# Position tile laid out with the table index outermost: column terms of a relative-position bias read back in 1 KB runs

## The chip, the cores and the metric

The kernel runs on one core of a Trainium2 chip. The metric is the device time of one execution in microseconds (us); less is better. A core has TensorE (PE) for matmuls, with its weight loads shown apart (PEld), VectorE (DVE), ScalarE (ACT), GpSimd (POOL), and SyncE (SP), which here only issues transfers. Transfers are carried by 16 DMA engines that all issuing queues share.

## What is computed

Two layers of attention with relative positions, each over 4 images of 32 x 32 positions and 768 channels, 12 heads of 64. For every layer (the first has no qkv bias and no scale on q inside the position terms; otherwise the same):

```
x   = x + attention(groupnorm(x))              # 32 groups of 24 channels
qkv = xn @ Wqkv (+ bias)                       # q, k, v: (B*12, 1024, 64)
rel_h[q=(h,w), kh] = q . Rh[h - kh + 31]       # table of 63 rows of 64
rel_w[q=(h,w), kw] = q . Rw[w - kw + 31]
scores = scale * q @ k.T + rel_h[..., :, None] + rel_w[..., None, :]
out = softmax(scores) @ v @ Wproj + bproj
```

The row term rel_h depends on the query's row h and the key's row; the column term rel_w on the query's column w and the key's column. In the second layer the tables have 27 rows, and the host's table is widened to 63 columns by repeating its edge.

## The kernel before

Everything is float32. The outer order is image by image, layer by layer (8 images in all), in an image the 6 pairs of heads (48 pairs, g), and in a pair 8 blocks of 128 queries (n = 0 to 7). A pair and a block is a unit of work: 384 of them, some 8.6 us each. The order of all instructions on all engines is written out by hand in the loop over the units; nothing is rescheduled. Matrix products for projections are split in Strassen's manner (products, values, combine, sums), which is why GpSimd subtracts weights (L133, L144) and adds inputs (L311).

In the iteration of unit u, in this order: SP issues what earlier iterations put off (the lists early and later); GpSimd computes the biases of unit u+2 (L521); TensorE computes the scores of u+1 (L535); VectorE adds score and bias and takes the row extreme (L547), ScalarE takes exponentials (L551); TensorE does a share of projections (L342, L370, L427) of the next pair; VectorE transposes the probabilities of u in blocks of 32 (L571) into tb, SP writes tb to a DRAM tile td (L573); VectorE takes reciprocals (L559) and ScalarE, in two of eight units GpSimd for one head, scales the probabilities of u+1 (L565, L563). One or two iterations later SP reads td back, turned, into pt (L582), and at n = 6 and at n = 2 of the next pair TensorE multiplies pt with v (L600, av). tb has two buffers, td five, sc six.

A matmul chain is split into two halves between which a small operation of VectorE or ScalarE on the weights (L331, L329) orders the halves.

Position terms, made twice a pair, half i for the blocks 4i to 4i+3 (96 halves in all):

- positions (L462): TensorE multiplies q of the pair with the table, 8 matmuls (L473), into a PSUM tile of (query, head h, block j, 128 table columns: 64 for rows, 64 for columns). ScalarE copies the 64 columns that belong to column terms into t (L478), and a window of the row columns into raw (L481). The PSUM tile comes from the pool ps_m, which has two buffers and also serves projections and av.
- place_positions (L486): ScalarE issues the write of t to a DRAM tile tdr (L488), 128 rows of 512 B per block, and copies raw into the row terms of the tile rel, four copies of 32 partitions (L496), for each of the four rows of a block of queries a window shifted by one.
- diagonals (L499), put off to a later iteration: for query column w the column terms are 32 table columns that begin at 31 - w. Reading tdr with a step between partitions of one row less one element turns that into a plain copy. Each read has 32 partitions, 4 blocks and 32 elements: runs of 128 B, 8 transfers (2 heads x 4 rows of queries) of 16 KB each, issued on SP (in the very first half four of them on ScalarE).
- biases (L514): for each head, row term plus column term, both repeated, to a full 128 x 1024 tile. Keys are kept in an order in which the column index splits into l (8) and a (4), so the column operand is read with a step of 4 elements (16 B).

SP's transfers and those of ScalarE use eight landing counters in turn: the program makes a transfer wait until the one that used its counter before, eight transfers earlier, has landed.

Of the kernel before, what the change touches and what calls it, by code (L numbers as in the profile page):

```python
# [31 lines left out]
FP = mybir.dt.float32  # L32
# [4 lines left out]
P = 128  # L37
B, HW, C = 4, 32, 768
S = HW * HW
# [6 lines left out]
HALF = 512  # L46
# [5 lines left out]
WIDE = HW + 4  # L52
# [4 lines left out]
def attention_blocks(ctx: ExitStack, tc: tile.TileContext, a: dict, out: bass.AP):  # L57
    nc = tc.nc
# [10 lines left out]
    tmppool = ctx.enter_context(tc.tile_pool(name="tmp", bufs=1))  # L69
    tbpool = ctx.enter_context(tc.tile_pool(name="tb", bufs=2))  # L70
    ptpool = ctx.enter_context(tc.tile_pool(name="pt", bufs=2))
    relpool = ctx.enter_context(tc.tile_pool(name="rel", bufs=3))
# [5 lines left out]
    dram2 = ctx.enter_context(tc.tile_pool(name="scratch2", bufs=2, space=bass.MemoryType.DRAM))  # L78
# [78 lines left out]
    for sign, base in ((1, 0), (-1, GS // NC - 1)):  # L157
        nc.gpsimd.affine_select(
            out=same_group, in_=same_group, pattern=[[-sign * (GS // NC), NG], [0, GS // NC]],
# [15 lines left out]
    for l in range(LAYERS):  # L175
        tab = const.tile([P, 2, 2 * HW], FP, tag=f"tab{l}", name=f"tab{l}")
        nc.gpsimd.memset(tab, 0.0)
        for i, ax in enumerate("hw"):
            src = a[f"rel{ax}{l}"]
            n = src.shape[1]  # L180
# [10 lines left out]
    for l in range(LAYERS):  # L191
        t = const.tile([P, NC], FP, tag=f"bo{l}", name=f"bo{l}")
# [121 lines left out]
    qk_of, v_of, rel_of, t_of = {}, {}, {}, {}  # L314
# [33 lines left out]
    def products(g, kind):  # L348
# [44 lines left out]
        if kind == 0:  # L393
            nc.scalar.copy(kept, ts[0])
            add(turned(qs[0]), ts[1], kept, 0)
            early_positions.append(lambda: positions(g, 0))
        elif kind == 1:
            add(ks[0], ts[0], kept)
            add(ks[1], ts[1], ks[0])
        elif kind == 2:  # L400
            add(turned(qs[1]), ts[1], ks[1], 0)
            add(ks[0], ts[0], ks[0])
            add(ks[1], ts[0], ks[1], 1)
        else:
            add(ks[0], ts[0], ks[0], 1)
            add(ks[0], ts[1], ks[0])
            if g + 1 < NPAIR:
                later.append(lambda: load_w(g + 1, "c"))
# [53 lines left out]
    def positions(g, i):  # L462

        l = images[g // NP][0]
        q = qk_of[g, 0]
        if i == 0:
            t_of[g] = dram2.tile([S, P], FP, tag="tdr", name=f"tdr_{g}")
        ps = ps_m.tile([P, 2, 4, P], FP, tag="m", name=f"tp_{g}_{i}")
        for j in range(4):
            for h in range(2):  # L470
                rows = slice(h * D, (h + 1) * D)
                at = 4 * i + j
                nc.tensor.matmul(  # L473
                    ps[:, h, j, :], lhsT=q[rows, at * P : (at + 1) * P], rhs=tabs[l][rows, :],
                    start=True, stop=True,
                )
        t = tmppool.tile([P, 4, 2, 2 * HW], FP, tag="tmp", name=f"t_{g}_{i}")
        nc.scalar.copy(t, ps[:, :, :, 2 * HW :].rearrange("p h j r -> p j h r"))  # L478
        raw = tmppool.tile([P, 2, 4, WIDE], FP, tag="raw", name=f"raw_{g}_{i}")
        first = ps[:, :, 0, 2 * HW - WIDE - 4 * 4 * i : 2 * HW - 4 * 4 * i]  # L480
        nc.scalar.copy(  # L481
            raw, bass.AP(first.tensor, first.offset, [first.ap[0], first.ap[1], [P - 4, 4], [1, WIDE]])
        )
        return lambda: place_positions(g, i, t, raw)

    def place_positions(g, i, t, raw):  # L486

        nc.scalar.dma_start(  # L488
            out=t_of[g][i * HALF : (i + 1) * HALF, :].rearrange("(j p) r -> p j r", p=P),
            in_=t.rearrange("p j h r -> p j (h r)"),  # L490
        )
        rel = relpool.tile([P, 2, 2, 4, HW], FP, tag="rel", name=f"rel_{g}_{i}")
        rel_of[g, i] = rel
        for y in range(4):
            rows = slice(y * HW, (y + 1) * HW)
            nc.scalar.copy(rel[rows, :, 0, :, :], raw[rows, :, :, WIDE - 1 - HW - y : WIDE - 1 - y])  # L496
        later.append(lambda: diagonals(g, i))

    def diagonals(g, i):  # L499
        td = t_of[g]  # L500
        for h in range(2):
            for y in range(4):
                src = bass.AP(
                    td.tensor, td.offset + (4 * i * P + HW * y) * P + h * 2 * HW + HW - 1,
                    [[P - 1, HW], [P * P, 4], [1, HW]],
                )
                (nc.scalar if h and not g + i else nc.sync).dma_start(
                    out=rel_of[g, i][y * HW : (y + 1) * HW, h, 1, :, :], in_=src
                )


    sc_of, st_of, tb_of, pt_of, attn_of = {}, {}, {}, {}, {}

    def biases(g, n):  # L514
        rel, m = rel_of[g, n // 4], n % 4
        for h in range(2):
            sc = scpool.tile([P, HW, HW], FP, tag="sc", name=f"sc_{g}_{n}_{h}")
            sc_of[g, n, h] = sc

            shape = [P, 4, HW, 8]  # L520
            nc.gpsimd.tensor_tensor(  # L521
                sc.rearrange("p (a k) (u l) -> p a (k u) l", a=4, l=8),
                rel[:, h, 0, m, :].unsqueeze(1).unsqueeze(3).to_broadcast(shape),
                rel[:, h, 1, m, :].rearrange("p (l a) -> p a l", a=4).unsqueeze(2).to_broadcast(shape),
                ALU.add,
            )

# [247 lines left out]
    with tc.manual_schedule(engines=ENGINES):  # L775
# [31 lines left out]
        load_w(1, "a")  # L807
        now["G3"].part()
        positions(0, 1)()
        run(later)  # L810
        run(later)
        ahead = prepare(1)
        fetch(3)
        biases(0, 0)
        scores(0, 0)()
        ahead["G0"].part()
        ahead["G0"].between()
        divide(0, 0)
        biases(0, 1)
        held = []  # L820
        same = {
# [10 lines left out]
        for at, (g, n) in enumerate(units):  # L832
# [37 lines left out]
            if at + 2 < len(units):  # L870
                biases(*units[at + 2])
# [3 lines left out]
            if n == 7 and g + 1 < NPAIR:  # L875
                placing.append(positions(g + 1, 1))
# [118 lines left out]
```

## Time and profile before

| | |
|---|---|
| median of 3 runs | 3310.84 us (3309.95 to 3312.62) |
| the profiled execution | 3317.11 us, of which the span of instructions is 3314.9 us |
| mean granted clock of TensorE | 1.0 |
| busy share | PE 99%, DVE 77%, POOL 72%, ACT 60% |
| transfers | 1047.38 MB in 524,180 packets, 316 GB/s; SP's and ScalarE's queue together take 89% of 16 DMA engines |
| diagonal reads (rel<-tdr) | 764 on SP and 4 on ScalarE, 16 KB each, 4.2 us from issue to landing (median on SP) |
| write of t (tdr<-t) | 96 on ScalarE, 256 KB each, 6.4 us to landing |

A group line has the kernel's line, engine, operation, what is written and read with shapes, and the count; after the first bar the busy time in us and the mean of one in ns; after the second the engine's idle time just before such instructions and what ended it. A row of waits has who waited for whom, the total in us, how many times, and the longest. SPq is SP's queue. Matmuls overlap in pairs, so a mean of one is longer than its share of the busy time. A busy TensorE says that a matmul is under way, its end is modelled.

### The profile page before, as it was taken

Reading aid. Unit: us, or ns where it says so; the run is one execution under the profiler, and the core shown is the slowest. Engines: PE = TensorE matmul, PEld = TensorE weight load, DVE = VectorE, ACT = ScalarE, POOL = GpSimd, SP = SyncE. Lnnn points to the kernel's source line nnn. Section 1 sums busy time; section 2 is a strip of 40 time slices with the busy share of each in tenths; the row PEclk is TensorE's granted clock in tenths of the full one; section 3 lists DMA queues with packets and bytes.
Section 4 is the critical chain, followed back from the end, with each engine's and each line's share of the span. In section 5 each row is a group of like instructions: output and inputs, shape, how many; then the busy total and the mean of one; then the engine's idle time right before and its main releaser. Section 6 shows DMA issues by size and latency. Waiting matters only on the chain.

```text
span 3314.9 us, 64967 instructions
## 1 busy us (share of the span) xinstructions
PE 3271.2 (99%) x25060; PEld 1884.7 (57%) x25060; DVE 2548.7 (77%) x4091; ACT 1998.0 (60%) x2997; POOL 2385.2 (72%) x1259
## 2 busy tenths in 40 slices
PE   7999999999999999999999999999999999999998
PEld 5566555655555555555555555655555555655554
DVE  5887778877788777777777877777777777777775
ACT  4666655666556665566656666556656566565653
POOL 7777866679676796677867778677786777767762
PEclk9999999999999999999999999999999999999999
DMA  4999999998998898898988999898998999898987
GB/s 151 329 332 325 325 330 321 322 331 321 331 322 318 317 329 310 314 331 310 336 313 316 332 324 329 307 336 309 331 333 305 328 319 324 316 327 297 330 288 269
DMA packets 524180, 1047.38 MB, mean 316 GB/s; under 512 B 139104, under 2 KB 202080, under 8 KB 474720
## 3 DMA queue, kind: packets, MB, share of 16 engines
q1 hardware_dynamic: 471552, 1015.90, 86.3%
q10 hardware_dynamic: 52320, 27.34, 2.8%
q8 instruction: 198, 3.24, 0.4%
q14 instruction: 110, 0.90, 0.1%
HBM read 568.00 MB, written 475.09 MB: 315 GB/s over the span
## 4 chain that ended last, share of the span: by engine, by line
PE 89%; DMA 7%; DVE 2%; issue 1%; POOL 1%; SPq 1%; ACT 0%; DVEq 0%; POOLq 0%; ACTq 0%
PE pj L342 21%; PE s L535 18%; PE av L600 18%; PE oo L342 13%; PE pv L342 11%; DMA td<-tb 4%; PE pj L370 3%; PE tp L473 2%; PE pv L427 2%; DMA pt<-td 1%; DVE tb L571 1%; PE o L679 1%; DMA xn<-in_x 1%; POOL sc L521 1%; DMA xn<-mid 0%
## 5 line engine op out<-in xcount | busy, mean ns | idle before, releaser
L521 POOL TENSOR_TENSOR sc<-rel 128x1024 f32<-128x1024 f32 x768 | 1878.5, 2477 | 476.5 <-DVE tb L571 456.1
L547 DVE CUSTOM_DVE_ANT_0 sc<-s,sc 128x1024 f32<-128x1024 f32 x768 | 910.9, 1223 | 349.0 <-PE s L535 287.0
L565 ACT ACTIVATE sc<-sc,sm 128x1024 f32<-128x1024 f32 x674 | 743.5, 1144 | 657.1 <-DVE sm L559 506.8
L551 ACT ACTIVATE sc<-sc,sm 128x1024 f32<-128x1024 f32 x768 | 878.5, 1146 | 343.9 <-DVE sm L547 342.4
L571 DVE STREAM_TRANSPOSE tb<-sc 128x1024 f32<-128x1024 f32 x768 | 908.4, 1223 | 75.5 <-DMA td<-tb 67.6
L535 PE MATMUL s<-k,q 64*128 64x512 f32 x3072 | 738.3, 596 | 1.9 <-DVE sm L547 1.3
L600 PE MATMUL av<-pt,v 128*64 128x256 f32 x6144 | 686.5, 381 | 11.5 <-DMA pt<-td 10.2
L600 PEld LDWEIGHTS av<-pt,v 128*64 128x64 f32 x6144 | 437.3, 137 | 290.1 <-issue 51.1
L342 PE MATMUL oo<-attn,wo 64*128 64x512 f32 x2112 | 475.3, 589 | 0.0
L535 PEld LDWEIGHTS s<-k,q 64*128 64x128 f32 x3072 | 284.8, 187 | 299.8 <-issue 267.0
L563 POOL TENSOR_SCALAR sc<-sc,sm 128x1024 f32<-128x1024 f32 x94 | 105.5, 1122 | 372.9 <-DVE sm L559 372.9
L342 PEld LDWEIGHTS oo<-attn,wo 64*128 64x128 f32 x2112 | 201.1, 187 | 227.8 <-issue 226.9
L342 PEld LDWEIGHTS pv<-wv,xn 64*128 64x128 f32 x4608 | 272.6, 188 | 35.3 <-issue 25.4
L342 PE MATMUL pv<-wv,xn 64*128 64x128 f32 x4608 | 275.0, 272 | 0.6 <-DVE wv L331 0.6
L342 PE MATMUL pj<-xn,wa 64*128 64x512 f32 x1152 | 268.9, 595 | 2.5 <-DVE xn L242 1.5
L342 PE MATMUL pj<-xn,w 64*128 64x512 f32 x1152 | 263.5, 589 | 0.0
L342 PE MATMUL pj<-s,w 64*128 64x512 f32 x576 | 262.7, 589 | 0.6 <-DVE v L444 0.6
L342 PE MATMUL pj<-s,wc 64*128 64x512 f32 x576 | 262.7, 589 | 0.0
L342 PEld LDWEIGHTS pj<-xn,wa 64*128 64x128 f32 x1152 | 113.6, 188 | 138.3 <-issue 125.1
L342 PEld LDWEIGHTS pj<-xn,w 64*128 64x128 f32 x1152 | 112.5, 187 | 134.9 <-issue 133.0
L444 DVE TENSOR_TENSOR v<-pv,v 128x512 f32<-128x512 f32 x216 | 140.1, 686 | 61.2 <-ACT v L446 44.2
L496 ACT COPY rel<-raw 32x256 f32<-32x256 f32 x384 | 155.0, 404 | 23.0 <-DMA part<-res 11.5
(95 smaller groups left out, 2642.5 us busy)
## 6 DMA issues: line engine op xcount, KB each, us to landing
td<-tb SPq DMA_DIRECT2D x384, 1024.0 KB, 6.5
pt<-td SPq DMA_DIRECT2D x382, 1024.0 KB, 8.8
tdr<-t ACTq DMA_DIRECT2D x96, 256.0 KB, 6.4
part<-res SPq DMA_DIRECT2D x84, 256.0 KB, 5.0
res<-part SPq DMA_DIRECT2D x84, 256.0 KB, 4.6
wa<-in_wqk SPq DMA_DIRECT2D x48, 384.0 KB, 3.2
wc<-in_wqk SPq DMA_DIRECT2D x48, 384.0 KB, 7.2
wv<-in_wv SPq DMA_DIRECT2D x24, 768.0 KB, 12.8
```

The costliest lines, as they stand in the source:

```text
L342: nc.tensor.matmul(to, lhsT=w, rhs=x, start=at == half == 0, stop=at == 0 and half == 1)
L370: nc.tensor.matmul(t[:, h, :], lhsT=w[rows, c, :], rhs=x[c][rows, :], start=(c == 0), stop=(c == NB - 1),)
L444: add = lambda to, x, y: nc.vector.tensor_tensor(to, x, y, ALU.add)
L496: nc.scalar.copy(rel[rows, :, 0, :, :], raw[rows, :, :, WIDE - 1 - HW - y : WIDE - 1 - y])
L521: nc.gpsimd.tensor_tensor(sc.rearrange("p (a k) (u l) -> p a (k u) l", a=4, l=8), rel[:, h, 0, m, :].unsqueeze(1).unsqueeze(3).to_broadcas ...
L535: nc.tensor.matmul(ps[h][:, cols], lhsT=q[rows, n * P : (n + 1) * P], rhs=k[rows, cols], start=True, stop=True,)
L547: nc.vector.tensor_tensor_reduce(out=sc, in0=ps[h], in1=sc, scale=-scale, scalar=BIG, op0=ALU.add, op1=ALU.min, accum_out=st[:, 0, h : h + 1],
L551: nc.scalar.activation(sc, sc, AF.Exp, bias=st[:, 0, h : h + 1], scale=-1.0, accum_out=st[:, 1, h : h + 1],)
L563: nc.gpsimd.tensor_scalar(sc, sc, st[:, 2, h : h + 1], 1.0, ALU.mult, ALU.mult)
L565: nc.scalar.mul(sc, sc, st[:, 2, h : h + 1])
L571: nc.vector.transpose(tb[:, :, h, :], sc_of[g, n, h])
L600: nc.tensor.matmul(av[rows, at * 2 * P : (at + 1) * 2 * P], lhsT=v_of[g][:, k, rows], rhs=pt_of[g, quarter].rearrange("p n r k h i -> p (n ...
```

## The change

The column terms are kept in another order at every step. The copy t has the table column r outermost and head and block innermost: (query, r, h, j), 512 elements of a query in one row of tdr, which becomes 256 rows of 512 elements. The write of t has one run of 2 KB per partition where it had four of 512 B. A query's column terms are then 32 x 8 = 256 elements in one run of 1 KB, and the diagonal step is 512 - 8 elements; both heads come in one transfer, 4 for a half pair in place of 8. The tile rel keeps its size and is used as two halves: row terms as before, but contiguous, and turned, with the column terms in the order (l, a, h, j). The bias operand of L521 is read from turned: its inner step is 32 elements (128 B) where it was 4 (16 B). Shapes, counts and the order of all other instructions stay.

```diff
@@ positions
-            t_of[g] = dram2.tile([S, P], FP, tag="tdr", name=f"tdr_{g}")
+            t_of[g] = dram2.tile([2 * P, HALF], FP, tag="tdr", name=f"tdr_{g}")
...
-        t = tmppool.tile([P, 4, 2, 2 * HW], FP, tag="tmp", name=f"t_{g}_{i}")
-        nc.scalar.copy(t, ps[:, :, :, 2 * HW :].rearrange("p h j r -> p j h r"))
+        t = tmppool.tile([P, 2 * HW, 2, 4], FP, tag="tmp", name=f"t_{g}_{i}")
+        nc.scalar.copy(t, ps[:, :, :, 2 * HW :].rearrange("p h j r -> p r h j"))
...
@@ place_positions
-            out=t_of[g][i * HALF : (i + 1) * HALF, :].rearrange("(j p) r -> p j r", p=P),
-            in_=t.rearrange("p j h r -> p j (h r)"),
+            out=t_of[g][i * P : (i + 1) * P, :], in_=t.rearrange("p r h j -> p (r h j)")
         )
-        rel = relpool.tile([P, 2, 2, 4, HW], FP, tag="rel", name=f"rel_{g}_{i}")
-        rel_of[g, i] = rel
+        both = relpool.tile([P, 2, 2, 4, HW], FP, tag="rel", name=f"rel_{g}_{i}")
+        rel, turned = both[:, 0], both[:, 1].rearrange("p h j r -> p (h j r)")
+        rel_of[g, i] = rel, turned
         for y in range(4):
             rows = slice(y * HW, (y + 1) * HW)
-            nc.scalar.copy(rel[rows, :, 0, :, :], raw[rows, :, :, WIDE - 1 - HW - y : WIDE - 1 - y])
+            nc.scalar.copy(rel[rows], raw[rows, :, :, WIDE - 1 - HW - y : WIDE - 1 - y])
...
@@ diagonals
-        for h in range(2):
-            for y in range(4):
-                src = bass.AP(
-                    td.tensor, td.offset + (4 * i * P + HW * y) * P + h * 2 * HW + HW - 1,
-                    [[P - 1, HW], [P * P, 4], [1, HW]],
-                )
-                (nc.scalar if h and not g + i else nc.sync).dma_start(
-                    out=rel_of[g, i][y * HW : (y + 1) * HW, h, 1, :, :], in_=src
-                )
+        for y in range(4):
+            src = bass.AP(
+                td.tensor, td.offset + (i * P + HW * y) * HALF + (HW - 1) * 8,
+                [[HALF - 8, HW], [1, 8 * HW]],
+            )
+            (nc.scalar if y % 2 and not g + i else nc.sync).dma_start(
+                out=rel_of[g, i][1][y * HW : (y + 1) * HW], in_=src
+            )
...
@@ biases
-        rel, m = rel_of[g, n // 4], n % 4
+        (rel, turned), m = rel_of[g, n // 4], n % 4
+        turned = turned.rearrange("p (l a h j) -> p h j a l", a=4, h=2, j=4)
...
-                rel[:, h, 0, m, :].unsqueeze(1).unsqueeze(3).to_broadcast(shape),
-                rel[:, h, 1, m, :].rearrange("p (l a) -> p a l", a=4).unsqueeze(2).to_broadcast(shape),
+                rel[:, h, m, :].unsqueeze(1).unsqueeze(3).to_broadcast(shape),
+                turned[:, h, m].unsqueeze(2).to_broadcast(shape),
```

## The prediction

> **What bounds the kernel now.** I read the page's busy shares first, then the waits of TensorE and of SP's queue, then two short timelines at the longest stall in mid-run, and last the groups of ScalarE and GpSimd that the change edits. The shares, from the page:
>
> ```profile
> PE 3271.2 (99%) x25060; PEld 1884.7 (57%) x25060; DVE 2548.7 (77%) x4091; ACT 1998.0 (60%) x2997; POOL 2385.2 (72%) x1259
> ...
> DMA packets 524180, 1047.38 MB, mean 316 GB/s; under 512 B 139104, under 2 KB 202080, under 8 KB 474720
> ```
>
> TensorE is the bound: it idles 3314.9 - 3271.2 = 43.7 us in all, so no edit on another engine or queue can return more. Where that idle time lies, TensorE's waits between 60 and 3230 us (start and end left out) tell; the columns are us in total, times, longest:
>
> ```profile
> PE av L600 <- DMA pt<-td: 8.2, 8, 1.9
> PE tp L473 <- DVE wo L331: 4.0, 3, 1.5
> PE pv L342 <- DVE wv L331: 0.8, 2, 0.6
> ```
>
> Only two rows have to do with transfers. The first waits for transposed probabilities that come back from DRAM; in the second VectorE is late because its transposes wait for tb, which the td write has not left yet. Together 12.2 us. The rest of the 43.7 us is start (about 20 us) and end, which the change hardly touches.
>
> Why are pt and td late? SP issues them in a fixed order, and waits there for the landing of earlier transfers:
>
> ```profile
> SPq L582 <- DMA td<-tb: 138.7, 82, 9.0
> SPq L507 <- DMA td<-tb: 132.7, 80, 3.2
> ...
> SPq L507 <- DMA pt<-td: 69.4, 41, 3.9
> ```
>
> L507 is the diagonal read, which needs neither td nor pt. It waits because the built program uses eight landing counters in turn, so each transfer waits for the one eight before. Eight diagonal reads in a row therefore wait for eight large transfers, and hold the next pt read behind them. SP's timeline, then TensorE's, at the longest mid-run stall (start, duration, count at the end of a row):
>
> ```profile
> 1353.92 11.55 SPq L507 DMA_DIRECT2D rel<-tdr  x8
> 1365.57 0.38 SPq L119 DMA_DIRECT2D wa<-in_wqk  x1
> 1366.04 0.93 SPq L582 DMA_DIRECT2D pt<-td  x2
> ```
> ```profile
> 1370.38 3.67 PE L600 MATMUL av<-pt,v 128*64 128x256 f32 x32
> 1375.91 2.38 PE L600 MATMUL av<-pt,v 128*64 128x256 f32 x20 [1.86 <-DMA pt<-td]
> ```
>
> The eight reads took 11.55 us of the queue; the pt reads left at 1366.04, and TensorE stood 1.86 us. This is what the change can reach.
>
> [...] its packet records, grouped by size, have 98,309 of 128 B at 12.9 ns (10 bytes a ns), 51,456 of 512 B at 27.6 (19), 11,520 of 1536 B at 76.8 (20) and 257,280 of 2048 B at 93.5 (22). [...]
>
> **The change, part by part.** The groups of GpSimd and of ScalarE that it edits, each with those I measure it against (count | busy us, mean ns of one | idle before, releaser):
>
> ```profile
> L521 POOL TENSOR_TENSOR sc<-rel 128x1024 f32<-128x1024 f32 x768 | 1878.5, 2477 | 476.5 <-DVE tb L571 456.1 <-DMA rel<-tdr 19.7 <-DMA pt<-td 0.5
> ...
> L311 POOL TENSOR_TENSOR s<-xn,xn 128x512 f32<-128x512 f32 x48 | 60.9, 1276 | 2.0 <-DVE xn L242 0.9
> ...
> L133 POOL TENSOR_TENSOR w<-wc,w 128x384 f32<-128x384 f32 x48 | 48.3, 1006 | 0.0
> ```
> ```profile
> L478 ACT COPY t<-tp 128x512 f32<-128x512 f32 x96 | 55.9, 582 | 130.5 <-PE tp L473 130.5
> ...
> L394 ACT COPY q<-pj 128x512 f32<-128x512 f32 x48 | 28.0, 584 | 68.6 <-PE pj L342 68.6
> L446 ACT COPY v<-pv 128x512 f32<-128x512 f32 x24 | 13.5, 564 | 2.1 <-PE pv L342 2.1
> ```
>
> *Removed from SP's queue:* 4 of 8 reads in each of 96 half pairs, 384 issues at the 0.43 us median that the trace gives L507 = 165 us of issuing, and with each the place in the ring of eight: four fewer large transfers to wait for. In the example the fifth to eighth issue began at 1358.55, 1362.01, 1364.54 and 1365.17: with four reads, done at 1356.97, the pt reads are free of the diagonals 8.5 us sooner, though they must still wait for their own data and counters. They were 1.9 us late. The moved queue holds xn, wa, td and pt behind the diagonals; all move earlier, none later.
>
> *Removed from the 16 DMA engines:* reads were 98,304 x 12.9 ns / 16 = 79 us per engine; now 384 x 32 = 12,288 runs of 1 KB. No such packet is in the trace; between 27.6 (512 B) and 76.8 ns (1536 B) I take 52 ns: 40 us (21 to 59). Writes were 49,152 x 27.6 / 16 = 85 us; now 12,288 of 2 KB x 93.5 / 16 = 72 us. Sum 164 to 112: 52 us of 3315, 1.6 points of DMA share. It is off the path except where pt and td are late already.
>
> *ScalarE's copy t (L478)* now reads PSUM with a step of 512 B[...]. A step of 16 B cost 584 (L394) against 564 ns contiguous (L446), so I take 582 as before; bounds 564 and twice, 1164. It matters more than ScalarE's 60% suggest: TensorE's av (L600) at n = 2 needs the PSUM tile that this copy and raw (L481) release. In half the pairs raw ended at 1611.26 and av began at 1611.43, 1.82 us after its scores began, just as in the other half, where raw ended 0.72 us before av. So cover is nil in 24 pairs: x us more costs 24x. The four copies into rel keep 32x256 at 404 ns; they write contiguously now, which I cost at nothing on an engine with 343.9 us of waits at L551.
>
> *GpSimd's bias (L521):* from 384 to 512 elements a plain addition grows (1276 - 1006) / 128 = 2.11 ns per element, so 1024 would take 1276 + 512 x 2.11 = 2356. L521 takes 2477: 16-B steps and repeats cost 5%. Bounds after: 2356[...]. I take 2477. Its first addition of a half pair now waits for all four reads, not the first head's four; 32 KB each in 32 packets, landing sooner than eight did.
>
> **Sum.** Of the 12.2 us I count two thirds as gone, 8 us: those after a run of diagonals go, some are only the load of pairs that prefetch xn. 3317.1 (profiled execution: 3314.9 and 2.2 around) becomes 3309; the median, 3310.84, is 6.3 us below that execution, and with the same stalls gone becomes 3303, -0.24%. If the 6.3 us are themselves such stalls, less is left to win; that is the first rival.
>
> **The rivals.** *Hidden anyway* (25%): the transfers land sooner, but the stalls come from DMA engines that are 89% busy, and 1.6 points don't matter. For it: at 560 us the td write was issued at once and took 9 us to land. Gain 1 to 2 us: 3309. *All relief* (10%): every mid-run stall and the like within the busy time goes: -16 us, 3294. *GpSimd becomes late* (10%, the slower side): place, the six iterations in which sums (L311) and weight differences (L133) lie between biases; GpSimd ran there from 741.5 to 788.0 without a pause, then had a pause of 6 us to take up arrears. Twelve biases in that stretch: [...] It decides from about 3.0 us per bias. [...] *ScalarE's copy doubles* (5%): 24 x 0.58 = 14 us, which eats the gain: 3317. That the change doesn't do what it says is excluded: the built program has four transfers of 32x256.
>
> **How the numbers follow.** Forecast 50%, its own range 3299 to 3307; three quarters of it lie below 3304.2, the bound for 0.2% (about what a measurement of this kernel can tell from no change). Faster: 0.38 + 0.10 = 0.48. Same: 0.12 + 0.25 = 0.37. Slower: 0.15. The range, 3293 to 3318, leaves out a part of full relief (3%) and most of the slow cases (13%).
>
> **What would show it.** Right: L507's waits in SP's queue from 202 us to under 100, L600's wait for pt under 4 us, L521 at 2477 and L478 at 582 unchanged, packets down by 123,000 (the data runs counted above) or a few more. Wrong: L521 over 3 us, L478 over 0.8 us with TensorE's av waiting for raw, or pt waits that stay though SP issues sooner.

## The result and the profile after

| | before | changed |
|---|---|---|
| median of 6 runs, us | 3311.73 | 3298.77 |
| lowest to highest, us | 3307.13 to 3317.01 | 3297.77 to 3300.50 |
| profiled execution (its span), us | 3317.11 (3314.9) | 3299.91 (3298.2) |
| ratio of the medians | | 0.9962, 95% interval 0.9952 to 0.9972 |

Three of the six runs of before are those that stand ahead of the prediction. The changed kernel is faster by 12.96 us, 0.38%. Its runs also scatter less: 2.7 us where before had 9.9. That fits waiting that differs from run to run better than a constant amount of work. The scatter goes in part with TensorE's granted clock, the gain does not. Of the 59 runs of before that stand beside the experiments below, 36 show a mean clock of 1.0 (median 3311.75 us) and 23 one of 0.999 or 0.998 (3314.41 us). All 12 runs of the changed kernel, these six and six more below, show 1.0 (3298.72 us), so at the same clock the gain is still 13.0 us.

The page after, first the busy shares and the packets, then the group of GpSimd's biases:

```profile
PE 3267.2 (99%) x25060; PEld 1881.4 (57%) x25060; DVE 2554.0 (77%) x4091; ACT 1999.6 (61%) x2997; POOL 2444.0 (74%) x1259
...
DMA packets 395153, 1047.33 MB, mean 318 GB/s; under 512 B 34657, under 2 KB 60769, under 8 KB 345697
...
L521 POOL TENSOR_TENSOR sc<-rel 128x1024 f32<-128x1024 f32 x768 | 1937.5, 2557 | 422.5 <-DVE tb L571 408.9
```

TensorE idles 3298.2 - 3267.2 = 31.0 us (43.7 before), and its busy time is 4.0 us shorter: these two are the 16.7 us by which the spans differ. GpSimd got slower, 2477 to 2557 ns a bias, and nothing waits longer for it. ScalarE's copy t, from its groups, kept its duration (582 before):

```profile
L478 ACT COPY t<-tp 128x512 f32<-128x512 f32 x96 | 56.1, 585 | 160.4 <-PE tp L473 160.4
```

TensorE's waits between 60 and 3230 us (us in total, times, longest), the same view as in the prediction:

```profile
PE av L600 <- DMA pt<-td: 1.1, 1, 1.1
PE pv L342 <- DVE wv L331: 0.8, 2, 0.6
PE pj L342 <- DVE wa L331: 0.6, 1, 0.6
```

The wait for pt fell from 8.2 to 1.1 us, and tp's wait for VectorE (4.0) is gone. The waits of SP's queue say why; the diagonal read is now L506:

```profile
SPq L582 <- DMA td<-tb: 133.9, 87, 8.0
...
SPq L704 <- DMA td<-tb: 39.6, 26, 2.9
...
SPq L506 <- DMA tdr<-t: 28.1, 2, 23.8
...
SPq L506 <- DMA pt<-td: 6.2, 3, 3.3
```

Before, the diagonal read waited 132.7 us for td and 69.4 us for pt. The td row has vanished and the pt row is 6.2 us. The row of L582 stays, since a pt read needs the td that it reads. Part of the waiting has moved to transfers that come later, and costs nothing there that shows: the write of a result at L704, which had no such row before, waits 39.6 us for td. SP's timeline and then TensorE's, at the place that the prediction shows:

```profile
1342.16 3.28 SPq L506 DMA_DIRECT2D rel<-tdr  x4
1345.54 0.40 SPq L119 DMA_DIRECT2D wa<-in_wqk  x1
1346.47 2.90 SPq L582 DMA_DIRECT2D pt<-td  x2
1349.82 10.12 SPq L573 DMA_DIRECT2D td<-tb  x2
```
```profile
1357.39 1.88 PE L535 MATMUL s<-k,q 64*128 64x512 f32 x8
1359.20 7.13 PE L600 MATMUL av<-pt,v 128*64 128x256 f32 x64
```

Four reads take 3.28 us of the queue where eight took 11.55, and all 64 matmuls of av run in one piece. One more row belongs here, VectorE's wait for tb, the buffer that a td write must leave first. Before and after:

```profile
DVE tb L571 <- DMA td<-tb: 67.6, 34, 6.0
```
```profile
DVE tb L571 <- DMA td<-tb: 10.5, 4, 5.7
```

**Which of the eight reads wait.** The prediction said that all eight wait for large transfers. The trace of before is more exact. In its example SP issued, just ahead of the reads, the second pt read (1350.20 us), a td write (1352.68) and xn (1353.06). The transfers between 1350 and 1366 us had these times from issue to landing (last column, us):

```profile
pt<-td SPq DMA_DIRECT2D x1, 1024.0 KB, 11.8
td<-tb SPq DMA_DIRECT2D x1, 1024.0 KB, 11.8
...
xn<-mid SPq DMA_DIRECT2D x1, 256.0 KB, 12.1
```

They landed at 1362.0, 1364.5 and 1365.2, and the sixth, seventh and eighth read began at 1362.01, 1364.54 and 1365.17: each follows, within 0.05 us, the landing of the transfer eight issues before. The fifth, at 1358.55, follows the first pt read in the same way (issued at 1349.25, 9.3 us to landing). The first four reads meet counters of older transfers, nearly all landed. The last four meet the two pt reads, the td write and xn that have just left. Over the whole trace of before, from the times of issue and landing of all transfers of SP and ScalarE, the first read of a row waited 24 us in all (one wait at the start), the second to fourth 0, 2 and 4, the fifth to eighth 16, 26, 56 and 113 us. The sixth and seventh mostly meet a pt read, the eighth mostly a td write. SP stands in these waits, and what is queued behind stands with it: in the example the eighth read began at 1365.17 us, and only then went wa (1365.57), the pt reads (1366.04) and the next td write (1367.07).

### The profile page after: what moved, and what is told of

Read it like the earlier page. It is cut to its first block, busy times and chain, and to the rows that moved or that the text cites. A ratio compares the mean times of both kernels' runs of the same rounds, so it can differ in the third digit from the quotient of the medians.

```text
span 3298.2 us, 64295 instructions
## 1 busy us (share of the span) xinstructions
PE 3267.2 (99%) x25060; PEld 1881.4 (57%) x25060; DVE 2554.0 (77%) x4091; ACT 1999.6 (61%) x2997; POOL 2444.0 (74%) x1259
## 2 busy tenths in 40 slices
DMA packets 395153, 1047.33 MB, mean 318 GB/s; under 512 B 34657, under 2 KB 60769, under 8 KB 345697
## 4 chain that ended last, share of the span: by engine, by line
PE 96%; DMA 1%; DVE 1%; ACT 0%; issue 0%; POOL 0%; SPq 0%; DVEq 0%; ACTq 0%
PE pj L342 22%; PE s L535 20%; PE av L600 20%; PE oo L342 14%; PE pv L342 11%; PE pj L370 4%; PE tp L473 2%; PE pv L427 2%; DMA td<-tb 1%; PE o L679 1%; DVE tb L571 1%; DVE sc L547 0%; DMA wa<-in_wqk 0%; ACT sc L565 0%; DMA xn<-in_x 0%
## 5 line engine op out<-in xcount | busy, mean ns | idle before, releaser
L521 POOL TENSOR_TENSOR sc<-rel 128x1024 f32<-128x1024 f32 x768 | 1937.5, 2557 | 422.5 <-DVE tb L571 408.9
L571 DVE STREAM_TRANSPOSE tb<-sc 128x1024 f32<-128x1024 f32 x768 | 908.9, 1225 | 11.2 <-DMA td<-tb 10.5
L600 PE MATMUL av<-pt,v 128*64 128x256 f32 x6144 | 684.7, 381 | 2.6 <-DMA pt<-td 1.3
L600 PEld LDWEIGHTS av<-pt,v 128*64 128x64 f32 x6144 | 434.0, 137 | 282.6 <-issue 37.8
L342 PEld LDWEIGHTS pj<-xn,w 64*128 64x128 f32 x1152 | 112.3, 187 | 135.0 <-issue 133.1
L444 DVE TENSOR_TENSOR v<-pv,v 128x512 f32<-128x512 f32 x216 | 140.2, 686 | 58.5 <-ACT v L446 43.7
```

The costliest lines, as they stand in the source:

```text
L342: nc.tensor.matmul(to, lhsT=w, rhs=x, start=at == half == 0, stop=at == 0 and half == 1)
L444: add = lambda to, x, y: nc.vector.tensor_tensor(to, x, y, ALU.add)
L521: nc.gpsimd.tensor_tensor(sc.rearrange("p (a k) (u l) -> p a (k u) l", a=4, l=8), rel[:, h, m, :].unsqueeze(1).unsqueeze(3).to_broadcast(s ...
L571: nc.vector.transpose(tb[:, :, h, :], sc_of[g, n, h])
L600: nc.tensor.matmul(av[rows, at * 2 * P : (at + 1) * 2 * P], lhsT=v_of[g][:, k, rows], rhs=pt_of[g, quarter].rearrange("p n r k h i -> p (n ...
```

## The experiments

All were timed beside the kernel before, whose medians there were 3312.1 (19 runs), 3312.88 (31) and 3311.18 us (9). Theory: the gain is that of SP's queue, because fewer reads stand in a row. Rivals: fewer and longer packets; and, for the small price, GpSimd's steps.

**Eight reads of 1 KB runs.** The changed kernel, with each read cut into two of 16 partitions. Layout and data runs stay; the number of issues is that of before.

```diff
-        for y in range(4):
+        for y in range(8):
             src = bass.AP(
-                td.tensor, td.offset + (i * P + HW * y) * HALF + (HW - 1) * 8,
-                [[HALF - 8, HW], [1, 8 * HW]],
+                td.tensor, td.offset + (i * P + 16 * y) * HALF + (HW - 1 - y % 2 * 16) * 8,
+                [[HALF - 8, 16], [1, 8 * HW]],
...
```

> The changed kernel with each of its four diagonal reads split in two of 16 partitions: eight transfers of 16 KB a half pair as before, but in 1 KB runs. Theory A (the gain is SP's queue: eight reads in a row pass a ring of eight landing counters and hold the pt reads and td writes behind them): nearly all of the gain goes, 3309 to 3313 us. Theory B (the gain is the time of the DMA engines: 123,000 fewer packets): 3298 to 3300 us, as the changed kernel. If both count, between 3302 and 3307.

Measured: 3312.44 us, ratio 0.9997 (0.9989 to 1.0006). The whole gain is gone, though the runs are still of 1 KB. SP's waits:

```profile
SPq L506 <- DMA td<-tb: 133.1, 79, 3.1
SPq L582 <- DMA td<-tb: 129.3, 81, 8.4
SPq L506 <- DMA pt<-td: 63.9, 40, 3.8
```

133.1 and 63.9 us are close to the 132.7 and 69.4 of before. SP's timeline near the same place shows the old run of eight:

```profile
1347.68 10.14 SPq L506 DMA_DIRECT2D rel<-tdr  x8
1357.91 0.37 SPq L119 DMA_DIRECT2D wa<-in_wqk  x1
1358.38 0.93 SPq L582 DMA_DIRECT2D pt<-td  x2
```

The time is that of before, but TensorE loses it in part elsewhere. In the profiled execution (span 3309.3 us) it idles 37.2 us (43.7 before), and the two rows that held 12.2 us before hold 5.1:

```profile
PE tp L473 <- DVE wo L331: 2.7, 3, 1.2
PE av L600 <- DMA pt<-td: 2.4, 2, 1.9
```

It is also busy for longer, 3272.1 us (3267.2 in the changed kernel), at a mean granted clock of 0.999 where both profiles above show 1.0; over the span that is some 3.3 us of lost clock (an estimate from the rounded 0.999, so 1.7 to 5.0). That stalls brought the lower clock is not shown: before stood 1.86 us at 1374.05 and kept a clock of 1.0.

**Four reads of 128 B runs.** The other half: four transfers as in the change, but the table index innermost again in t, tdr and rel, so that a read has runs of 128 B and the bias operand steps 16 B.

```diff
-        nc.scalar.copy(t, ps[:, :, :, 2 * HW :].rearrange("p h j r -> p r h j"))
+        nc.scalar.copy(t, ps[:, :, :, 2 * HW :])
...
-                [[HALF - 8, HW], [1, 8 * HW]],
+                [[HALF - 1, HW], [2 * HW, 8], [1, HW]],
...
-        turned = turned.rearrange("p (l a h j) -> p h j a l", a=4, h=2, j=4)
+        turned = turned.rearrange("p (h j l a) -> p h j a l", a=4, h=2, j=4)
...
```

> The changed kernel with the table index kept innermost: the write of t in 2 KB runs and four transfers of 32 KB a half pair as in the changed kernel, but the diagonal is read in runs of 128 B, as before, and the bias operand with a step of 16 B. Theory A (SP's queue): 3298 to 3301 us. Theory B (time of the DMA engines): 3309 to 3313 us, since 98,304 packets of 128 B are back; a mean of a L521 addition near 2477 ns in place of 2557 is expected by both.

Measured: 3299.17 us, ratio 0.9960 (0.9946 to 0.9974): the full gain. A bias takes 2478 ns again, as both theories had it. Its page shows the small packets back (132,960 under 512 B, against 34,657):

```profile
DMA packets 481168, 1047.33 MB, mean 318 GB/s; under 512 B 132960, under 2 KB 146784, under 8 KB 431712
```

So the 98,304 short packets cost nothing that this kernel's time shows (3299.17 against 3298.68 us for the changed kernel timed beside it), and what matters in the change is that four transfers do the work of eight, not their runs of 1 KB. In the packet records of before, by size in the prediction, a packet of 128 B moves 10 bytes a ns (12.9 ns each) and those of 512 B and more 19 to 22; it doesn't follow that the time of this kernel depends on it.

**The step of the bias operand.** The column operand taken in six orders in turn, so that its inner step is 4, 8, 16, 32, 64 or 128 B; all else as changed. Only the last order takes the elements that belong there, so this kernel's values are not those of the reference.

```diff
+            which = (2 * n + h) % 6
+            if which == 0:
+                nc.gpsimd.tensor_tensor(to, row, col("a h j l"), ALU.add)
+            elif which == 1:
+                nc.gpsimd.tensor_tensor(to, row, col("a j l h"), ALU.add)
...
+            else:
+                nc.gpsimd.tensor_tensor(to, row, col("l a h j"), ALU.add)
```

> The changed kernel, but the column operand of the bias addition is taken in six other orders in turn, so that its inner step is 4, 8, 16, 32, 64 or 128 B; all but one order take the wrong elements, so the values are not those of the reference. If the price of the step grows with it, L521's six lines rise from about 2360 ns (4 B) by 2477 (16 B) to 2557 (128 B); if a step beyond 8 B has one price, four are alike. Time: GpSimd is off the path at either price, so 3297 to 3300 us; if GpSimd's 80 ns had cost something, 2 to 4 us less than the changed kernel's 3298.8.

Measured: 3297.93 us, ratio 0.9954 (0.9943 to 0.9966). GpSimd's groups; L528 steps 4 B, L530 8, L532 16, L534 32, L536 64, L538 128:

```profile
L534 POOL TENSOR_TENSOR sc<-rel 128x1024 f32<-128x1024 f32 x144 | 359.8, 2499 | 0.0
L532 POOL TENSOR_TENSOR sc<-rel 128x1024 f32<-128x1024 f32 x144 | 356.6, 2477 | 55.2 <-DVE tb L583 39.5 <-DMA rel<-tdr 15.8
L530 POOL TENSOR_TENSOR sc<-rel 128x1024 f32<-128x1024 f32 x144 | 284.9, 1978 | 0.0
L528 POOL TENSOR_TENSOR sc<-rel 128x1024 f32<-128x1024 f32 x144 | 281.4, 1954 | 244.0 <-DVE tb L583 244.0
L538 POOL TENSOR_TENSOR sc<-rel 128x1024 f32<-128x1024 f32 x96 | 245.0, 2553 | 0.0
L536 POOL TENSOR_TENSOR sc<-rel 128x1024 f32<-128x1024 f32 x96 | 238.1, 2480 | 242.9 <-DVE tb L583 242.9
```

In this addition there is a cliff, and it lies between 8 and 16 B: 1978 to 2477 ns, about 500 ns or 25%. Beyond it only the step of 128 B adds 3%. The 172 us less of additions than in the changed kernel (1937.5 less the six groups' 1765.8) bought under 1 us, inside the scatter: GpSimd isn't on the path.

**The changed kernel again**, beside these three.

> The changed kernel again, on the chip of the other three, as their measure: 3297 to 3301 us.

Measured: 3298.68 us, ratio 0.9957 (0.9945 to 0.9969).

**The eight reads of before, in two fours.** The kernel before with its own reads and layout. The first head's four go one iteration earlier, the second head's stay where they were.

```diff
-        later.append(lambda: diagonals(g, i))
+        diagonal_later.append(lambda: diagonals(g, i, 0))
+        later.append(lambda: diagonals(g, i, 1))
...
             run(behind[0])
             behind.append(behind.pop(0))
+            run(diagonal_early)
+            diagonal_early, diagonal_later = diagonal_later, diagonal_early
```

> The kernel before, its eight diagonal reads of a half pair kept as they are (16 KB, runs of 128 B), but in two groups of four that are issued an iteration apart: the first head's right after the pt reads of the iteration ahead, the second head's where all eight were. Theory C (what costs is the run of more than four in a row, which meets the landing counters of large transfers just issued): 3298 to 3303 us, with L507's waits for td and pt near zero. Theory D (what costs is the number of reads, by their issue time on SP and their places in the ring): 3308 to 3313 us.

Measured: 3299.51 us, ratio 0.9961 (0.9947 to 0.9974). The full gain comes with not one transfer fewer and not one byte moved otherwise (524,181 packets). SP's timeline:

```profile
1339.10 1.82 SPq L507 DMA_DIRECT2D rel<-tdr  x4
1341.03 0.47 SPq L573 DMA_DIRECT2D td<-tb  x1
1341.92 0.34 SPq L103 DMA_DIRECT2D xn<-mid  x1
1344.54 5.00 SPq L507 DMA_DIRECT2D rel<-tdr  x4
1349.64 0.38 SPq L119 DMA_DIRECT2D wa<-in_wqk  x1
1350.12 1.30 SPq L582 DMA_DIRECT2D pt<-td  x2
```

Its waits show a surprise:

```profile
SPq L507 <- DMA pt<-td: 178.3, 102, 4.3
...
SPq L507 <- DMA tdr<-t: 83.2, 34, 23.5
```

The td row is gone, as I expected, but the reads wait longer for pt than before (178.3 against 69.4 us), which I had not, and it costs nothing. (The first head's reads, being earlier, also wait more often for the write of t.) A wait of the reads themselves isn't the harm, then. What is left is which transfers stand behind it, and when these could have gone.

**All eight reads earlier.** The kernel before with its eight reads one iteration earlier, in one row, behind that iteration's pt reads and ahead of the next td write. The list diagonal_later is run one iteration before later, as in the experiment above.

```diff
-        later.append(lambda: diagonals(g, i))
+        diagonal_later.append(lambda: diagonals(g, i))
...
             run(behind[0])
             behind.append(behind.pop(0))
+            run(diagonal_early)
+            diagonal_early, diagonal_later = diagonal_later, diagonal_early
```

> The kernel before, all eight reads of a half pair issued together but an iteration earlier, ahead of a td write that VectorE releases late, so that several transfers lie between them and the next pt reads. If it only matters what is queued closely behind the eight reads, most of the gain comes: 3299 to 3304 us. If eight in a row do the same harm there, 3308 to 3313 us.

Measured: 3308.59 us, ratio 0.9987 (0.9980 to 0.9993). SP's and VectorE's waits:

```profile
SPq L507 <- DMA pt<-td: 418.3, 178, 4.0
```
```profile
DVE tb L571 <- DMA td<-tb: 55.7, 26, 9.4
```

The reads wait 418 us, and the td write stands behind them: VectorE's wait for tb hardly falls (67.6 to 55.7 us), and a third of the gain comes.

**All eight reads behind the pt reads.** The kernel before with its reads in their own iteration still, but after the pt reads that they stood ahead of. Three lists in rotation make the call come one iteration later than above.

```diff
-        later.append(lambda: diagonals(g, i))
+        diagonal_later.append(lambda: diagonals(g, i))
...
             run(behind[0])
             behind.append(behind.pop(0))
+            run(diagonal_early)
+            diagonal_early, diagonal_next, diagonal_later = (
+                diagonal_next, diagonal_later, diagonal_early
+            )
```

> The kernel before, all eight reads of a half pair in the same iteration as before, but behind its pt reads and not ahead of them. The pt reads are no longer held, while the td write that follows is: if TensorE's stalls come from held pt reads alone, 3299 to 3303 us; if the td writes matter as much, 3305 to 3312 us.

Measured: 3305.20 us, ratio 0.9980 (0.9970 to 0.9990). Half of the gain, with no read fewer and nothing ahead of pt; the td writes still stand behind.

**Six reads.** The changed kernel with two of its four reads halved.

```diff
-        for y in range(4):
+        for at, n in (0, HW), (HW, HW), (64, 16), (80, 16), (96, 16), (112, 16):
...
```

> The changed kernel with two of its four reads split in two, so six a half pair: between four (3298.8 us) and eight (3312.4 us). Theory C: the fifth and sixth wait for large transfers, the harm is more than half there or begins here, 3303 to 3310 us with L506's waits for td from near zero to some 60 to 100 us. Theory D (harm by number): halfway, 3305 to 3306 us, with waits of half the size.

Measured: 3303.43 us, ratio 0.9970 (0.9959 to 0.9981), between four and eight. By the order of the counters in the example the fifth and sixth read meet those of the two pt reads, and only wa (L119) behind them that of the td write. Its waits agree:

```profile
SPq L506 <- DMA pt<-td: 23.5, 14, 3.5
SPq L119 <- DMA td<-tb: 15.6, 9, 2.3
```

The 60 to 100 us for which theory C had the reads wait for td didn't come; they wait 4.4 us for it.

**Two and two.** The changed kernel with its four reads in two groups an iteration apart.

```diff
-        later.append(lambda: diagonals(g, i))
+        diagonal_later.append(lambda: diagonals(g, i, (0, 1)))
+        later.append(lambda: diagonals(g, i, (2, 3)))
...
```

> The changed kernel with its four reads in two groups of two, an iteration apart, as the eight were split before: does shortening the row further bring anything? If what costs is a row longer than the queue can take, four is short enough and the time is that of the changed kernel, 3297.5 to 3300 us. If every read in a row costs its share (1.7 us from four to eight is 13.6 us, so 3.4 us a read), 3290 to 3294 us.

Measured: 3298.47 us, ratio 0.9963 (0.9949 to 0.9976): nothing beyond the change. (Where the expectation gives 1.7 us from four to eight reads, that is a slip; eight cost 13.8 us more than four, by the first and the fourth experiment.)

All in one view, in order of time; the waits are of the one profiled execution of each:

| kernel | reads in a row | time, us | ratio | DVE waits for td to leave tb, us |
|---|---|---|---|---|
| eight of 1 KB runs | 8 | 3312.44 | 0.9997 | 46.3 |
| before | 8 | 3311.73 | 1 | 67.6 |
| eight earlier | 8 | 3308.59 | 0.9987 | 55.7 |
| eight behind pt | 8 | 3305.20 | 0.9980 | 31.1 |
| six | 6 | 3303.43 | 0.9970 | 23.4 |
| two by four | 4, 4 | 3299.51 | 0.9961 | 16.3 |
| four of 128 B runs | 4 | 3299.17 | 0.9960 | 12.0 |
| changed | 4 | 3298.77 | 0.9962 | 10.5 |
| two and two | 2, 2 | 3298.47 | 0.9963 | 10.4 |

The four kernels with at most four in a row lie within 1.1 us, wherever the reads stand. Six in a row cost 4.7 us more than the changed kernel and eight, where they stood before, 13 to 14. The order of the times is nearly that of VectorE's wait. "Eight of 1 KB runs" breaks it (46.3 us at the longest time): a total of waits in one execution doesn't say how much of each reached TensorE.

## Why the prediction was right, and where it was off

**The mechanism held.** The reads in a row hold SP's queue by their landing counters; with four of them pt and td leave earlier, and TensorE's stalls go. The experiments isolate it from both sides: packets without the row (four of 128 B runs) give all, the row without the old packets (eight of 1 KB runs) gives nothing. Both of these write t in runs of 2 KB, and two by four has the full gain with the old write, so the write isn't it either. The prediction put the waits of the diagonal read at under 100 us from 202; they are 6 us for td and pt. It put av's wait for pt at under 4 us; it is 1.1.

**One statement of it was too coarse.** Not eight reads wait for eight large transfers, but the last four for those just issued. (And in its example xn stands ahead of the reads, not behind them.) From that it would have followed that two fours do as well as the change, with no new layout.

**The size was off: "two thirds of 12.2 us, 8 us".** Measured in the same two rows of TensorE's waits: 8.2 to 1.1 and 4.0 to none, 11.1 of 12.2 us; little of it was, as the prediction had it, "only the load of pairs that prefetch xn". Second, the rows didn't hold everything: the spans differ by 16.7 us. The prediction left out the end of the span, "which the change hardly touches", but the same wait stands there too, from 3230 us on, before and after:

```profile
PE av L600 <- DMA pt<-td: 2.0, 2, 1.5
```
```profile
PE av L600 <- DMA pt<-td: 0.2, 1, 0.2
```

Another 4.0 us had been inside what counts as busy, 1.8 of them in av's matmuls (L600, 686.5 to 684.7 us; they start in pairs, some 7 ns apart, and each takes 381 ns on average both times). Two by four, with the layout of before, is busy for only 3265.9 us (3271.2 before), so this belongs to the queue, not to the layout. Together these make up the 16.7 us to within 0.2. Third, the other way: the profiled execution of before was a bad one of its kind, 5.4 us above the median, that of the changed kernel 1.1 above. From 17.2 us between the two executions this takes 4.2 and leaves the 13.0 us between the medians. The prediction saw this danger ("if the 6.3 us are themselves such stalls, less is left to win"), and the wide scatter of before fits it; but the two terms above outweighed it. The errors partly cancel, so that 3303 came as near as it did is in part luck. The result lies 0.2 us below the forecast's own range of 3299 to 3307, and half way to "all relief" (3294), which describes the profiled pair well: 17.2 us against its 16.

**The rivals.** "Hidden anyway" fell: the stalls came from the order of the queue, not from busy DMA engines (two by four has the full gain while SP's and ScalarE's queue take 91.1% of them, more than the 89.1% of before). The 52 us less per DMA engine that the prediction worked out weren't to be had as time, which it had said ("off the path except where pt and td are late already"); they don't even stand out in the share of SP's and ScalarE's queue, 89.1% both times. The packet records say where they went: the 49,264 packets of 8 KB took 359.9 ns each on average where they had taken 339.7, which is 62 us more per engine; why they took longer is open. The 1 KB packets took 54.7 ns on average where I had put 52. "GpSimd becomes late" fell: a bias takes 2557 ns, under the 3.0 us from which it would decide (an estimate: 2477 ns and the pause of 6 us shared by twelve biases), and its cover holds for 80 ns. That a bias could come to more than 3.0 us was the author's estimate, which no trace showed; of the six steps measured the slowest takes 2553 ns. "ScalarE's copy doubles" fell: 585 ns against 582, so the step of 512 B is nearly free; that it could cost twice was likewise the author's estimate.

**What I costed wrongly without harm.** L521 was to stay at 2477 ns; the step of 128 B costs 80 ns more. The sentence that steps and repeats cost 5%, with a floor of 2356 ns, was wrong: I had extrapolated from additions that stream two operands (2.11 ns an element), while L521, with its repeated row term, takes 1954 ns at a step of 4 B; that the repeat makes it cheaper wasn't tested. At 16 B the cliff was paid before the change already: the 499 ns from 8 to 16 B are 0.49 ns for each of 1024 elements. Why the price rises there no run shows. Packets fell by 129,027: the 122,880 data runs, and 16 for each of the 384 transfers that went (6,144), all but three. (Eight of 1 KB runs has 384 transfers and 6,147 packets more than the changed kernel.)

**What stays open.** How the gain splits between the pt reads and the td write is told only by three cases (behind pt: half; ahead of td: a third; six: three quarters), and these overlap. A third buffer for tb, which might free VectorE without touching the queue, wasn't tried. What brings the lower clock of some executions, and how much of the scatter it makes, is open too. No version beat the changed kernel by more than the scatter.

## What to carry to other kernels

Count how many transfers a queue issues in a row against the number of landing counters, and look at what they meet: here, with eight counters, small transfers waited for the large ones that had left just before them (113 us in all at the eighth read of a row) and held the urgent ones behind. Before a layout is rebuilt for longer runs, try the same transfers in smaller groups at other places in the order; here that alone gave all of the gain. And read a stall view of a part of the span as a lower bound, and the scatter of the runs as a hint: 12.2 us in two rows became 16.7 us of span, and runs that differed by 10 us came to lie within 3.

## What the runs showed of the hardware that was not expected

- A wait of 178 us (two by four) or 418 us (eight earlier) in SP's queue cost nothing in the one kernel and two thirds of the gain in the other; the total says little, and what differs is what is queued behind.
- 98,304 packets of 128 B in place of 12,288 of 1 KB, with DMA engines about 90% busy, made no difference in time: 3299.17 against 3298.77 us.
- GpSimd's 128x1024 addition with a repeated operand takes 1954 ns at a step of 4 B, 1978 at 8, 2477 at 16, 2499 at 32, 2480 at 64 and 2553 at 128.
- ScalarE's copy of 128x512 from PSUM takes 585 ns with a step of 512 B, 584 ns with the table index left innermost (runs of 64).
